# A planned instruction order: searched while the kernel is built, or replayed from a row of stored choices

## The chip, the cores and the metric

The kernel runs on one core of a Trainium2 chip. The metric is the device time in microseconds. TensorE (PE) does the matmuls, VectorE (DVE), ScalarE (ACT) and GpSimd (POOL) the elementwise work, and SyncE (SP) issues most of the transfers. "PEld" in the profile is the weight load of a matmul, which overlaps the matmul before it.

## The reference

The input is 128 graphs of 64 nodes with 256 features (`x`), a 0/1 adjacency of 64 x 64 per graph, and a node mask. Four layers follow one another, and each has the form `x = layernorm(x + layer(x, adj))`:

```python
# layer 0: five rounds of a gated unit
A = (adj != 0)
for l in range(5):
    m   = h @ weight[l]
    agg = einsum('bij,bid->bjd', A, m)
    r, z = sigmoid(...), sigmoid(...)        # of agg @ w_ih.T + h @ w_hh.T + biases
    n    = tanh(i_n + r * h_n)
    h    = (1 - z) * n + z * h
# layer 1: sum over neighbours, W1 (256 -> 1024), RMS norm, silu, W2 (1024 -> 256)
# layer 2: log map, sum over neighbours, exponential map, projection into the ball
# layer 3: attention weights exp(e_i + f_j) masked by adj, normalised, times h = x @ W_w.T + W_b
```

All arithmetic is in float32.

## The kernel before

Two graphs of 64 nodes fill the 128 partitions, with a block-diagonal 128 x 128 adjacency (`edge`). Four such pairs make a group of 8 graphs, and there are 16 groups, numbered 0 to 15. A group goes through all four layers without leaving the chip: load `x`, five gated rounds, then layer 1, 2 and 3, and a store of 512 KB. Nothing passes between groups. Large buffers exist in three sets (`NF = 3`, group number modulo 3), so that a few groups are in flight at any time, at different points of their chain.

The order of the instructions isn't the order of the program text. The functions below only *describe* operations: each call of `flow.op` or `flow.either` records an engine (or two possible engines), an estimated time, the buffers read and written, and a closure that will emit the instruction. A group's operations form one stream. After all streams are described, `Flow.issue` makes a plan: it simulates the five engines with those estimated times and takes, again and again, the operation that could start first among the next few of each stream on each engine. Where several could start at the same time, a ranking decides. There are four rankings: the older stream first; the younger stream first, except for transfers; and two that weigh the length of the chain that still hangs on the operation against the stream's number (`LAGS`, 60 and 150).

The search is over rankings. The planned time is cut into stretches of 37.5 us (`STRETCH`), 10 us near the end (`LAST_STRETCH`). For each stretch every surviving plan is copied and continued with each of the four rankings, and the best 8 (32 near the end) survive by a lower bound of the end (`bound`). The best plan at the end is emitted, with a dependency that keeps each engine in the planned order. Each engine works through its own instructions in that order, and waits for others by semaphores.

Names for the steps that follow:
- `gated` is one round of layer 0. `new_state` (L843) ends it for half of the group: L845 and L847 are two DVE instructions of 128 x 512 that write the new state `hT` (`hN` in the code). `rows_of` (L655) turns the state back into rows on PE, into the bank `ps_hr`; after the fifth round this gives `y0` (L893) and the layer norm that ends layer 0.
- A layer norm has `st`, `mv` and `ve` on DVE, a power on GpSimd (`rstd`, L690), `off` on DVE, and the scaled rows `x_n` on ACT or DVE (L365, L366).
- At the start of layer 1, `aggm` is `x_n` summed over neighbours, and `xb` (L909) is `x_n` plus a bias, 128 x 1024, on GpSimd. The four differences `t` (L934) on DVE feed the products of layer 1. The last two groups (14 and 15) use plain products `ps_hid` in place of these.
- Layer 1 then has the squares `sq` and their sum `sqs`, `ps_ss` and `ps_rms` on PE, scaled and passed through silu into `hid` (L996 on DVE, L998 on ACT), and the product `ps_o`.
- Layer 2 has the factor `fac` and `tan` (L1046), the product `ps_sup`, the squares `junk_a` (L1057), the tanh `th` (L1063) and `y2` (L1079). Layer 3 has `ps_T`, `ps_a`, `hw`, `ps_att`, `rd` and `y3` (L1112).
- `copied` and `scaled` are the operations that either ACT or DVE can do; the plan picks the engine.

Two of the descriptions, with their estimated times:

```python
xb = rows("y", "xb")
pool(2.35, lambda: nc.gpsimd.tensor_tensor(xb.tile(), x1.tile(), over(b2_r.tile(), NB), OP.add), [xb], [x1, b2_r])
# new_state
dve(512, lambda: nc.vector.scalar_tensor_tensor(
    hN[:, :, half(n)], z.tile(), 1.0, hN[:, :, half(n)], OP.add, OP.mult), [(hN, n)], [(hN, n), z])
```

Of the kernel before, what the change touches and what calls it, by code (L numbers as in the profile page):

```python
# [26 lines left out]
class Buf:  # L27


    def __init__(self, make, slot=None, bank=False):  # L30
        self.make, self.slot, self.bank = make, slot, bank
        self.ap, self.uses, self.left, self.after = None, [], 0, ()
# [10 lines left out]
class Op:  # L43
    __slots__ = ("eng", "us", "run", "ways", "stream", "n", "kb", "sets", "need", "then", "bufs", "opens", "id", "way")

    def __init__(self, ways, stream, n, kb, sets):
        self.ways = {eng: (us, run) for eng, us, run in ways}
        self.eng, self.us, self.run = ways[0]
        self.stream, self.n, self.kb, self.sets = stream, n, kb, sets
        self.need, self.then, self.bufs, self.opens, self.id, self.way = 0, [], (), None, 0, 0.0  # L50


class Plan:


    def __init__(self, flow):
        self.flow = flow
        ops = [o for s in flow.streams for o in s]
        self.need = [o.need for o in ops]
        self.at = [0.0] * len(ops)  # L60
        self.uses = {}
        self.clock = dict.fromkeys(flow.AHEAD, 0.75)
        self.queues = [{e: deque(o for o in s if e in o.ways) for e in self.clock} for s in flow.streams]
        self.banks = [0.0] * BANKS
        self.left, self.first, self.bus, self.done = len(ops), 0, 0.0, 0.0
        self.lands = [0.0] * flow.TRANSFERS
        self.past, self.order, self.table = None, [], None

    def copy(self):
        c = Plan.__new__(Plan)  # L70
        c.flow, c.need, c.at, c.uses = self.flow, self.need.copy(), self.at.copy(), self.uses.copy()
        c.clock, c.banks, c.lands = self.clock.copy(), self.banks.copy(), self.lands.copy()
        c.queues = [{e: d.copy() for e, d in q.items()} if self.first <= s < self.first + 2 * self.flow.WINDOW else q
                    for s, q in enumerate(self.queues)]
        c.left, c.first, c.bus, c.done = self.left, self.first, self.bus, self.done
        c.past, c.order, c.table = (self.past, self.order), [], self.table
        return c

    def advance(self, until, rank):


        flow, need, at, clock, banks = self.flow, self.need, self.at, self.clock, self.banks
        while self.left and clock["PE"] < until:
            best = None
            for s in range(self.first, min(self.first + flow.WINDOW, len(self.queues))):
                for e, q in self.queues[s].items():
                    opened = False
                    for _, o in zip(range(flow.AHEAD[e]), q):
                        t = max(clock[e], at[o.id])
                        if o.opens is not None:  # L90
                            if opened or not banks or need[o.id]:
                                opened = True
                                continue
                            t = max(t, banks[0])
                        elif need[o.id]:
                            continue
                        elif o.kb and e != "POOL":
                            t = max(t, self.lands[0])
                        elif o.sets and self.table not in o.sets:
                            t += flow.TABLE  # L100
                        key = (t + flow.SOONER if len(o.ways) > 1 and e == "DVE" else t, *rank(s, o))
                        if best is None or key < best[0]:
                            best = key, o, e, t
            if best is None:
                return False
            _, o, eng, t = best
            if o.sets and self.table not in o.sets:
                self.table = o.sets[0]
            for e in o.ways:
                self.queues[o.stream][e].remove(o)  # L110
            self.order.append((eng, o))
            end = t + o.ways[eng][0]
            clock[eng] = end
            if eng == "PE":
                self.done += o.us
            if o.opens is not None:
                banks.pop(0)
            for b in o.bufs:
                n = self.uses.get(b, b.left) - 1
                self.uses[b] = n  # L120
                if not n:
                    banks.append(end + flow.hop(eng, "PE"))
                    banks.sort()
            if o.kb:
                self.bus = max(self.bus, end + flow.DMA[0]) + o.kb / flow.DMA[1]
                end = self.bus + flow.DMA[2]
                if o.eng != "POOL":
                    self.lands = [*self.lands[1:], end]
            for u in o.then:
                need[u.id] -= 1  # L130
                at[u.id] = max(at[u.id], end + flow.hop(eng, u.eng))
            self.left -= 1
            while self.first < len(self.queues) and not any(self.queues[self.first].values()):
                self.first += 1
        return True

    def bound(self):

        now = self.clock["PE"]
        end = max(now - self.done + self.flow.work, *self.clock.values())  # L140
        for q in self.queues[self.first:]:
            for d in q.values():
                if d:
                    end = max(end, max(self.at[d[0].id], now) + d[0].way)
        return end


class Flow:
# [20 lines left out]
    TRANSFERS = 8  # L169

    TABLE = 1.28
    WINDOW, STRETCH, WIDTH, LAGS = 4, 37.5, 8, (60.0, 150.0,)


    ENDGAME, LAST_STRETCH, LAST_WIDTH = 400.0, 10.0, 32

    BEHIND = mybir.DependencyInfo(mybir.DependencyClass.NoSync, mybir.DependencyReason.DATA)

# [7 lines left out]
    def op(self, eng, us, run, w=(), r=(), kb=0, sets=None):  # L186
        self.either([(eng, us, run)], w, r, kb, sets)

    def either(self, ways, w, r, kb=0, sets=None):

        o = Op(ways, len(self.streams) - 1, len(self.ops), kb, sets)
        before = set()
        for accesses, writes in ((r, False), (w, True)):
# [34 lines left out]
    def ways(self):  # L228

        for i, o in enumerate(o for s in self.streams for o in s):  # L230
            o.id = i
        path = {}
        for ops in self.streams:
            longest = 0.0
            for o in reversed(ops):
                path[o] = o.us + max((path[u] + self.hop(o.eng, u.eng) for u in o.then if u.stream == o.stream), default=0.0)
                o.way = longest = max(longest, path[o])
        self.work = sum(o.us for ops in self.streams for o in ops if o.eng == "PE")

    def issue(self):  # L240
        self.ways()
        ranks = (lambda s, o: (s, o.n), lambda s, o: (s if o.kb else -s, o.n), *(lambda s, o, lag=lag: (lag * s - o.way, s, o.n) for lag in self.LAGS))
        plans, until = [Plan(self)], 0.0
        while any(p.left for p in plans):
            late = until > self.work - self.ENDGAME
            until += self.LAST_STRETCH if late else self.STRETCH
            found = {}
            for p in plans:
                for rank in ranks:
                    c = p.copy()  # L250
                    if c.advance(until, rank):
                        found.setdefault((round(c.bound(), 3), c.left), c)
            plans = [found[k] for k in sorted(found)[:self.LAST_WIDTH if late else self.WIDTH]]
        p, parts = plans[0], []
        past = (p.past, p.order)
        while past is not None:
            parts.append(past[1])
            past = past[0]
        last = {}
        for part in reversed(parts):  # L260
            for eng, o in part:
                made = o.ways[eng][1]()
                for i in made if isinstance(made, list) else [made]:
                    if eng in last:
                        self.tc.add_manual_dep(i.ins, last[eng].ins.name, self.BEHIND, reason="the plan's order")
                    last[eng] = i


@with_exitstack
# [884 lines left out]
```

## Time and profile before

| what | value |
|---|---|
| time, median of three runs | 2415.85 us (2415.77 to 2416.1) |
| span of the profiled execution | 2413.2 us |
| instructions in it | 32774 |
| mean granted TensorE clock | 0.993 of full speed |
| DMA | 36.22 MB, a mean of 15 GB/s |

The page of the profile gives busy times by engine, the span in 40 slices, the chain of work that ended last, and groups of instructions with what they waited for. In a row of the timeline the columns are start in us, duration in us, engine, line, operation, output and inputs with their shape, a count where several were merged, and in brackets how long the engine had stood idle before it and which instruction released it. A row of the waits reads: who waited, for whom, us in total, how often, and the longest.

### The profile page before, as it was taken

To read this page: it belongs to the slowest core of one execution; us is meant where nothing else is said; L and a number is where in the kernel's file an instruction comes from. 1 tells how busy PE (TensorE), PEld (TensorE's weight loads), DVE (VectorE), ACT (ScalarE), POOL (GpSimd) and SP (SyncE) were. 2 spreads that over 40 slices of the span, in tenths; PEclk is the share of its full clock that TensorE was granted. 3 is DMA by queue.
4 is the path that set the end of the run, shared out by engine and by line. 5 is a ranking of instruction groups with operands and counts; after the bars stand their busy time and mean duration, and the time that the engine had idled before them with its cause. 6 is when DMAs were issued, how large, how long until landed. Compare 5 with 4: busy or idle time off the path is not lost.

```text
span 2413.2 us, 32774 instructions
## 1 busy us (share of the span) xinstructions
PE 2364.1 (98%) x12098; PEld 2071.5 (86%) x12098; DVE 1894.3 (78%) x4404; ACT 1211.1 (50%) x2549; POOL 175.1 (7%) x144
## 2 busy tenths in 40 slices
PE   9999999999999999999999999999999999999995
PEld 7888888888888888888888888888888888888764
DVE  5677887878869787887977877878697987888766
ACT  3344554545544555555454455455454544555454
POOL 2000000000000000000000000000010000100001
PEclk9999999999999999999999999999999999999997
DMA  3000000000000000000000000000000000000000
GB/s 121 10 9 3 1 29 1 27 3 1 29 1 29 1 18 12 1 29 1 27 3 1 27 3 4 26 1 29 1 18 12 27 3 1 27 10 18 10 9 18
DMA packets 39727, 36.22 MB, mean 15 GB/s; under 512 B 9956, under 2 KB 38656, under 8 KB 39568
## 3 DMA queue, kind: packets, MB, share of 16 engines
q1 hardware_dynamic: 37840, 32.25, 4.2%
q8 instruction: 96, 1.57, 0.3%
q10 hardware_dynamic: 1328, 1.31, 0.2%
q0 software_dynamic: 400, 0.57, 0.1%
q14 instruction: 63, 0.52, 0.1%
HBM read 25.74 MB, written 8.39 MB: 14 GB/s over the span
## 4 chain that ended last, share of the span: by engine, by line
PE 91%; DVE 6%; ACT 1%; issue 1%; POOL 0%; POOLq 0%; ACTq 0%; DVEq 0%
PE p_v L772 11%; PE p_r L772 11%; PE p_w L772 11%; PE p_in L675 11%; PE ps_o L342 9%; PE ps_agg L342 6%; PE p_hy L783 6%; PE p_u L772 6%; PE p_hx L783 4%; PE ps_hr L655 3%; PE ps_a L342 2%; PE p_wh L938 2%; PE p_vh L938 2%; PE p_1h L938 2%; PE ps_sup L342 1%; PE ps_hid L342 1%
## 5 line engine op out<-in xcount | busy, mean ns | idle before, releaser
L675 PE MATMUL p_in<-agg,w_in 128*128 128x256 f32 x1280 | 321.3, 379 | 0.0
L675 PEld LDWEIGHTS p_in<-agg,w_in 128*128 128x128 f32 x1280 | 242.2, 190 | 33.9 <-issue 1.0
L342 PE MATMUL ps_o<-w2s,hid 128*128 128x256 f32 x1024 | 234.0, 381 | 4.8 <-ACT hid L998 4.8
L342 PEld LDWEIGHTS ps_o<-w2s,hid 128*128 128x128 f32 x1024 | 193.8, 191 | 32.4 <-ACT hid L998 5.9
L690 POOL TENSOR_TENSOR rstd<-ve,pow 128x4 f32<-128x4 f32 (+1 forms) x64 | 83.6, 1306 | 1407.3 <-DVE ve L688 1401.3
L826 ACT ACTIVATE V<-V,half_b 128x256 f32<-128x256 f32 x160 | 73.3, 500 | 195.4 <-DVE V L822 195.4
L772 PE MATMUL p_v<-tA,w_h 128*128 128x256 f32 x640 | 170.0, 379 | 0.5 <-DVE V L822 0.5
L772 PE MATMUL p_r<-hT,w_h 128*128 128x256 f32 x640 | 168.5, 379 | 0.0
L772 PE MATMUL p_v<-tB,w_a 128*128 128x256 f32 x640 | 167.1, 379 | 0.0
L772 PE MATMUL p_r<-agg,w_a 128*128 128x256 f32 x640 | 167.0, 380 | 0.0
L794 DVE SCALAR_TENSOR_TENSOR hnb<-p_hy,half_b,hs 128x256 f32<-128x256 f32 x240 | 108.6, 478 | 46.1 <-PE p_hy L783 45.2
L342 PEld LDWEIGHTS ps_agg<-edge,hr 128*128 128x128 f32 x1024 | 136.8, 191 | 8.2 <-ACT hr L360 0.5
L342 PE MATMUL ps_agg<-edge,hr 128*128 128x128 f32 x1024 | 138.7, 275 | 0.0
L360 ACT COPY agg<-ps_agg 128x512 f32<-128x512 f32 x154 | 89.1, 579 | 98.7 <-PE ps_agg L342 98.2
L360 ACT COPY hr<-ps_hr 128x512 f32<-128x512 f32 x125 | 72.2, 578 | 128.2 <-PE ps_hr L655 127.7
L772 PEld LDWEIGHTS p_v<-tB,w_a 128*128 128x128 f32 x640 | 120.7, 190 | 16.1 <-DVE tB L759 0.2
L772 PEld LDWEIGHTS p_r<-agg,w_a 128*128 128x128 f32 x640 | 119.1, 190 | 15.9 <-issue 0.5
L772 PEld LDWEIGHTS p_v<-tA,w_h 128*128 128x128 f32 x640 | 118.4, 190 | 15.9 <-DVE V L822 1.4
L783 PE MATMUL p_hy<-tA,w_hn 128*128 128x256 f32 x480 | 131.3, 380 | 0.0
L772 PEld LDWEIGHTS p_r<-hT,w_h 128*128 128x128 f32 x640 | 116.6, 190 | 14.0 <-PE ps_hr L655 0.5
L826 ACT ACTIVATE Z<-Z,half_b 128x256 f32<-128x256 f32 x160 | 73.8, 503 | 93.4 <-DVE Z L822 93.2
L826 ACT ACTIVATE U<-U,half_b 128x256 f32<-128x256 f32 x160 | 73.3, 500 | 88.9 <-DVE U L822 88.4
(242 smaller groups left out, 5346.9 us busy)
## 6 DMA issues: line engine op xcount, KB each, us to landing
x<-in_x_dram SPq DMA_DIRECT2D x16, 512.0 KB, 3.6
xr<-in_x_dram SPq DMA_DIRECT2D x16, 512.0 KB, 3.5
out_dram<-x_n SPq DMA_DIRECT2D x16, 512.0 KB, 2.9
edge<-in_adj_dram SPq DMA_DIRECT2D x32, 64.0 KB, 2.3
wm<-in_L_gnn_weight_dram SPq DMA_DIRECT2D x5, 256.0 KB, 5.3
w2s<-in_L_gnn_W_dram SPq DMA_DIRECT2D x1, 1024.0 KB, 9.1
w<-in_L_gnn_W_dram SPq DMA_DIRECT2D x2, 512.0 KB, 3.4
w_in_L_gnn_w_hh_dram<-in_L_gnn_w_hh_dram ACTq DMA_DIRECT2D x1, 512.0 KB, 5.2
```

The costliest lines, as they stand in the source:

```text
L342: return nc.tensor.matmul(o, lhsT, rhs, start=(k == 0), stop=(k == nk - 1))
L360: flow.either([("ACT", 0.22 + 0.00077 * n, lambda: nc.scalar.copy(o(), i())), ("DVE", 0.145 + 0.00105 * n, lambda: nc.vector.tensor_copy(o ...
L655: turn(lambda j=j, c=c: nc.tensor.transpose(ps[:, j * D + c * P:j * D + (c + 1) * P], src[:, c, (2 * n + j) * P:(2 * n + j + 1) * P], iden ...
L675: pe(256, lambda c=c, k=k: nc.tensor.matmul(ps[:, c * HR:(c + 1) * HR], w[:, k, c * P:(c + 1) * P], v(k), start=first and c == k == 0, sto ...
L690: pool(1.1, lambda: nc.gpsimd.tensor_tensor(rstd[:, :m, :], ve[:, :m, :], pow2[:, :m, :], OP.pow), [rstd], [ve])
L772: pe(256, lambda i=i, w=w, c=c: nc.tensor.matmul(ps[:, c * HR:(c + 1) * HR], w[:, m, c * P:(c + 1) * P], v[i][0](), start=first and i == 1 ...
L783: pe(256, lambda: nc.tensor.matmul(ps[:, j * HR:(j + 1) * HR], w_hn[:, m, :], v[1][0](), start=first, stop=True, skip_group_check=True), [ ...
L794: dve(300, lambda: nc.vector.scalar_tensor_tensor(o[0](), ps[:, j * HR:(j + 1) * HR], b(c), x[0](), OP.add, OP.add), [o[1]], [ps, x[1], ha ...
L826: act(256, lambda c=c: nc.scalar.activation(o[:, c, :], src(c), AF.Tanh, bias=half_b[:, i * KD + c:i * KD + c + 1], scale=0.5), [(o, c)], ...
L938: pe(256, lambda c=c: nc.tensor.matmul(ps[:, c * HR:(c + 1) * HR], w1f[:, w, (2 * q + c) * P:(2 * q + c + 1) * P], v[0](), start=first and ...
```

## The change

The search is taken out of the kernel. It was run beforehand, wider and with stretches of 6 us, and its outcome is a row of digits, one per stretch, each naming the ranking to use there. `issue` replays the row: one plan, advanced stretch by stretch with the named ranking, and emitted in the same way as before. What only the search needed (`copy`, `bound`, the counters) goes. The operations, their estimated times, the rankings and the buffers are unchanged. It spares the search when the kernel is built, and gives the search room that it did not have there.

```diff
 class Plan:
-        self.left, self.first, self.bus, self.done = len(ops), 0, 0.0, 0.0
+        self.left, self.first, self.bus = len(ops), 0, 0.0
...
-    def copy(self):
...
-    def bound(self):
...
 class Flow:
-    WINDOW, STRETCH, WIDTH, LAGS = 4, 37.5, 8, (60.0, 150.0,)
-
-
-    ENDGAME, LAST_STRETCH, LAST_WIDTH = 400.0, 10.0, 32
+    WINDOW, STRETCH, LAGS = 4, 6.0, (60.0, 150.0)
+    CHOICES = ("0110020220222022110000000000000120101020000001000000100001011101021010111100022010012111021102110212"
...
+               "112001001101000011110001101111010000101110212211001011110012111101101111002010001101101100101000001")
...
     def issue(self):
...
-        plans, until = [Plan(self)], 0.0
-        while any(p.left for p in plans):
-            late = until > self.work - self.ENDGAME
-            until += self.LAST_STRETCH if late else self.STRETCH
-            found = {}
-            for p in plans:
-                for rank in ranks:
-                    c = p.copy()
-                    if c.advance(until, rank):
-                        found.setdefault((round(c.bound(), 3), c.left), c)
-            plans = [found[k] for k in sorted(found)[:self.LAST_WIDTH if late else self.WIDTH]]
...
+        plan, until = Plan(self), 0.0
+        for c in self.CHOICES:
+            until += self.STRETCH
+            assert plan.advance(until, ranks[int(c)])
+        assert not plan.left
```

More of the change, by code (lines that the diff above doesn't have):

```diff
@@ L64, in __init__ @@
         self.banks = [0.0] * BANKS
-        self.left, self.first, self.bus, self.done = len(ops), 0, 0.0, 0.0
+        self.left, self.first, self.bus = len(ops), 0, 0.0
         self.lands = [0.0] * flow.TRANSFERS
-        self.past, self.order, self.table = None, [], None
-    def copy(self):
[L70 to L77, printed above, removed]
+        self.order, self.table = [], None
     def advance(self, until, rank):
@@ L113, in advance @@
             clock[eng] = end
-            if eng == "PE":
-                self.done += o.us
             if o.opens is not None:
@@ L135, in advance @@
         return True
-    def bound(self):
[L139 to L145, printed above, removed]
 class Flow:
@@ L171 @@
     TABLE = 1.28
-    WINDOW, STRETCH, WIDTH, LAGS = 4, 37.5, 8, (60.0, 150.0,)
-    ENDGAME, LAST_STRETCH, LAST_WIDTH = 400.0, 10.0, 32
+    WINDOW, STRETCH, LAGS = 4, 6.0, (60.0, 150.0)
+    CHOICES = ("0110020220222022110000000000000120101020000001000000100001011101021010111100022010012111021102110212"
+               "1120110110211100000000111110010001121220011022021210001010210110000020000222000000102020202020020121"
+               "1201200002000200002000000021200011121200100100211000010100011012002012000101100110200012101010102210"
+               "112001001101000011110001101111010000101110212211001011110012111101101111002010001101101100101000001")
     BEHIND = mybir.DependencyInfo(mybir.DependencyClass.NoSync, mybir.DependencyReason.DATA)
@@ L237, in ways @@
                 o.way = longest = max(longest, path[o])
-        self.work = sum(o.us for ops in self.streams for o in ops if o.eng == "PE")
     def issue(self):
@@ L242, in issue @@
         ranks = (lambda s, o: (s, o.n), lambda s, o: (s if o.kb else -s, o.n), *(lambda s, o, lag=lag: (lag * s - o.way, s, o.n) for lag in self.LAGS))
-        plans, until = [Plan(self)], 0.0
-        while any(p.left for p in plans):
-            late = until > self.work - self.ENDGAME
-            until += self.LAST_STRETCH if late else self.STRETCH
-            found = {}
-            for p in plans:
-                for rank in ranks:
-                    c = p.copy()
-                    if c.advance(until, rank):
-                        found.setdefault((round(c.bound(), 3), c.left), c)
-            plans = [found[k] for k in sorted(found)[:self.LAST_WIDTH if late else self.WIDTH]]
[L254 to L258, printed above, removed]
-        last = {}
[L260 to L266, printed above, removed]
+        plan, until = Plan(self), 0.0
[3 more added lines that the diff above has]
+        assert not plan.left
+        last = {}
+        for eng, o in plan.order:
+            made = o.ways[eng][1]()
+            for i in made if isinstance(made, list) else [made]:
+                if eng in last:
+                    self.tc.add_manual_dep(i.ins, last[eng].ins.name, self.BEHIND, reason="the plan's order")
+                last[eng] = i
 @with_exitstack
```

## The prediction

> **What bounds the kernel now.** First the row of busy times. TensorE (PE) is at 98%, the next engine, VectorE (DVE), at 78%.
>
> ```profile
> PE 2364.1 (98%) x12098; PEld 2071.5 (86%) x12098; DVE 1894.3 (78%) x4404; ACT 1211.1 (50%) x2549; POOL 175.1 (7%) x144
> ```
>
> The chain of waits agrees (PE 91% of it, DVE 6%). A change of order alone leaves these matmuls as they are, so it can win only what PE stands idle or runs at a lower clock. A table of four stretches (length; busy time of PE, PEld, DVE, ACT, POOL; granted clock; DMA) says where that lies:
>
> ```profile
> 0.00:100.00 100.00, 97.48 (x477) 79.36 (x478) 61.58 (x146) 36.17 (x83) 18.56 (x32) 1.00 0.26 79
> 100.00:2300.00 2200.00, 2188.26 (x11297) 1932.61 (x11296) 1764.17 (x4035) 1119.68 (x2355) 140.16 (x100) 1.00 0.04 12
> 2300.00:2362.50 62.50, 57.40 (x248) 43.78 (x247) 37.98 (x96) 32.38 (x53) 7.02 (x5) 0.97 0.03 9
> 2362.50:2413.20 50.70, 21.00 (x81) 15.78 (x79) 30.62 (x129) 22.87 (x59) 9.35 (x7) 0.69 0.06 21
> ```
>
> Idle PE is 2.5 us at the start, 11.7 us in the 2200 us of the middle, 5.1 us between 2300 and 2362.5 us, and 29.7 us after that, where the last two groups have only short matmuls between long vector chains. Of 49 us in all, most of the last 29.7 us cannot go. Now the waits of PE:
>
> ```profile
> PE ps_T L645 <- ACT x_n L365: 10.2, 1, 10.2
> PE ps_hr L655 <- DVE hT L847: 7.9, 9, 1.5
> PE ps_sup L342 <- ACT tan L1046: 5.9, 1, 5.9
> PE ps_o L342 <- ACT hid L998: 4.8, 2, 4.5
> ```
>
> Three are single waits at the end. The second is the middle: ps_hr waits for the last step of a new state, over and over. The timeline around one of them (start, duration, engine, line) shows why:
>
> ```profile
> 481.79 2.36 POOL L909 TENSOR_TENSOR xb<-x_n,b_r 128x1024 f32<-128x1024 f32 x1 [2.49 <-ACT x_n L365]
> ```
> ```profile
> 482.54 2.16 DVE L845 SCALAR_TENSOR_TENSOR hT<-U,hT 128x512 f32<-128x512 f32 x1 [0.51 <-ACT U L826]
> 484.73 0.69 DVE L847 SCALAR_TENSOR_TENSOR hT<-hT,R 128x512 f32<-128x512 f32 x1
> ```
> ```profile
> 485.57 0.63 PE L655 MATMUL ps_hr<-ident,hT 128*128 128x128 f32 x4 [0.96 <-DVE hT L847]
> ```
>
> L845 takes 2.16 us here and 0.69 us elsewhere. It ends 0.55 us after GpSimd's xb does, 1.47 us late; PE had work for about 0.5 us of that and stood 0.96 us. The plan prices L845 at the same 0.68 us everywhere, so it does not see this. The old plan repeats itself for most groups (these waits come some 145 us apart), and so hits the same spot each time. Last, the end:
>
> ```profile
> 2321.01 2.08 PE L342 MATMUL ps_o<-w2s,hid 128*128 128x256 f32 x4 [4.46 <-ACT hid L998]
> ...
> 2362.50 1.89 PE L342 MATMUL ps_sup<-tan,adjT 128*128 128x256 f32 x8
> 2370.31 3.78 PE L342 MATMUL ps_sup<-tan,adjT 128*128 128x256 f32 x8 [5.92 <-ACT tan L1046]
> 2384.26 2.16 PE L645 MATMUL ps_T<-ident,x_n 128*128 128x128 f32 x8 [10.16 <-ACT x_n L365]
> ```
> ```profile
> 2374.69 0.38 ACT L1057 ACTIVATE junk_a<-ps_sup 128x256 f32<-128x256 f32 x1
> ...
> 2375.19 1.28 ACT L1063 ACT_TABLE_LOAD   x1
> 2376.48 0.30 ACT L1063 ACTIVATE th<-n 128x4 f32<-128x4 f32 x2
> ```
>
> PE waits 4.46 us for group 14's hid, then after the last ps_o for each step of the two groups. ACT does both groups' tanh (th) together, behind group 15's four squares and a table load, though group 14's was ready far earlier.
>
> **What the Trainium skill says.** "SBUF — State Buffer", section "Who interferes with whom": a DVE instruction with two SBUF inputs contends with a GpSimd instruction that reads SBUF, and the later one is blocked until the first is done. L845 has two such inputs, xb too, and 2.16 against 0.69 us agrees. "TensorE: Matmul & The Clock Gate", Part 1: PE's clock is halved after an idle window of some 3.4 us. The trace agrees: the same eight ps_sup take 1.89 us before and 3.78 us after the 5.92 us wait. "ScalarE: Activation LUTs", section "What ACT_TABLE_LOAD costs": about 1283 ns for a load; the trace has 1283 ns.
>
> **The change, part by part.** The search leaves the build and a row of 399 digits picks the rule for each 6 us stretch. By the order of instructions on each engine, built for both kernels, work is neither added nor removed: 6596 matmuls as written in both, 46 table loads in both, and 17 either-engine operations move from DVE (4401 to 4384) to ACT (2490 to 2507). At 0.4 to 0.7 us each that is some 9 us of 1894 us, hidden under PE. The search cost the device nothing. What stays is where things stand.
>
> (a) Start: the first 21 rows on PE are the same; the 2.5 us stay. Further on, most of the first two layers' weight products (ps_wmih) come earlier, in a stretch where PE has no idle time: 0.
>
> (b) Middle. In the old order the pair L845, L847 stands directly ahead of a group's first t<-aggm (L934) in 8 of 14 groups, which is the collision: 8 waits of ps_hr, 7.6 us of the 11.7 us. In the new order it stands there in 3. At 0.95 us each these still cost 2.9 us. The other 11 groups also have one xb each, which will hit some other DVE instruction. In the old trace the six groups outside the pattern lost the rest, 4.1 us or 0.69 us a group, part of it other small misses. I take 0.5 us for each of the eleven, a little under that, since a search with shorter stretches should leave PE more ready work: 5.5 us. Middle 8.4 us, a gain of 3.3 us. Bounds: at 0.69 us the gain is 1.2 us; with nothing lost at the eleven it is 8.8 us.
>
> (c) The wait for hid. In the old order group 14's ps_o had only a few transposes of group 15 beside it. Idle there is 4.46 + 0.26 + 0.30 us and the slower clock after it makes 4 matmuls and 16 ps_agg take 2.08 + 2.56 us instead of some 1.03 + 1.95 us: 6.7 us in all. In the new order both groups' ps_hid come first, 13 of group 15's stand between group 14's ps_ss and ps_rms, and ps_ss of group 15 follows. Then PE waits for group 15's last copy, square and add (0.58 + 0.72 + 0.69 us, less 0.44 us of ps_rms): 1.6 us; and, as the silu table load (1.28 us) and first silu (0.72 us) stand behind that square on ACT, some 0.4 us more after ps_ss. With x_n of group 15 and its aggm copies between ps_hid (1 to 1.5 us) I take 3.4 us. Gain 3.3 us, from 1 to 6.
>
> (d) The last chain. The new order on ACT puts the table load and group 14's th ahead of group 15's squares, in the time PE needs for ps_sup. It can start when tan of group 15 is done, 2371.1 us on the old scale: load to 2372.3, th to 2372.5, six small DVE steps of 0.2 us to 2373.7, against 2377.9 us before: 4 us earlier, and with it group 14's ps_T, 10.16 us of wait. Behind it, group 15's chain gives part back: its x_n is now four ACT instructions behind group 14's hw (before: split between ACT and DVE), about 1 us, and x_n of group 14 stands late, so that both output transfers meet: some 0.5 us more. On DVE the block of 0.83 us before off of group 14 goes. I take 3.0 us, from 1 to 4.5.
>
> Sum: 3.3 + 3.3 + 3.0 = 9.6 us, 2415.85 to **2406.2 us**.
>
> **The rivals.** *Tail only:* every xb finds a victim again and the middle stays at 11.7 us. For it: 16 xb, 2.4 us each, and DVE at 78%. Against: six groups of the old trace lost less. 2415.85 − 6.3 = 2409.5 us. *Nearly everything goes:* the middle falls to 2 us, the hid wait to 1 us, the chain gains 4.5 us: 9.7 + 5.7 + 4.5 = 19.9 us, 2396 us. Against: the plan still prices no collision. *Slower:* the new order has no repeating pattern; groups stand closer together at times (reloads xr of groups 2 and 3 almost meet on the queue), so that it could lose in more places. If all 14 groups lost the longest wait seen, 1.48 us, and half of them a second of 0.96 us, the middle would be 27.4 us, 15.7 more; less 6.3 us at the end this gives 2425 us. Against: nothing in the old trace loses twice as a rule.
>
> **How the numbers follow.** Likeliest case 60%, tail only 15%, nearly everything 10%, slower 15%. The range 2396.5 to 2414.5 us leaves out half of the third case (5%) and the slower one (15%). Bound (0.2%): 2411.0 and 2420.7 us. Below it lie the first and third and two thirds of the second case, 80%; within it 9%, from the second and the milder part of the fourth; above it 11%.
>
> **What would show it.** After: PE busy time as before; ps_hr waiting for hT in about 3 places, not 9; idle in the middle near 8 us; a wait of ps_o for hid under 3 us and the clock at 1.00 there; th of group 14 before group 15's squares, and the wait of ps_T near 6 us. Wrong if the middle loses more than 12 us, by many small waits of PE for DVE or ACT, or if tail waits merely move from ps_T to the last group.

## The result and the profile after

The changed kernel takes **2407.89 us** (median of four runs, 2406.22 to 2409.2) where the kernel before, on the same chip, takes 2415.97 us (2415.77 to 2417.17). The ratio is 0.9966, with a 95% interval from 0.9952 to 0.998: 8.1 us, or 0.34%, faster. The forecast was 2406.2 us, with a range from 2396.5 to 2414.5 us. The profiled executions of the two differ by 9.1 us (2413.2 and 2404.1 us; that of the changed kernel is the fastest of its four runs), and the readings below account for those 9.1 us.

The lines of the changed kernel carry numbers 34 lower than those of the kernel before: L811 and L813 are the two steps of hT that were L845 and L847, L875 is xb, L900 is t, L611 the transposes ps_T, L1029 is th. First the row of busy times, which shows the same matmuls on an engine that is as busy as before:

```profile
PE 2362.7 (98%) x12098; PEld 2071.9 (86%) x12098; DVE 1886.2 (78%) x4387; ACT 1222.5 (51%) x2566; POOL 173.6 (7%) x144
```

Then the table of four stretches of the changed kernel (start and end; length; busy time and count of PE, PEld, DVE, ACT, POOL; granted clock; DMA share and GB/s):

```profile
0.00:100.00 100.00, 97.23 (x481) 79.66 (x482) 61.66 (x143) 38.30 (x86) 18.93 (x32) 1.00 0.26 78
100.00:2300.00 2200.00, 2188.88 (x11316) 1937.86 (x11315) 1757.83 (x4027) 1125.48 (x2365) 138.76 (x100) 1.00 0.04 12
2300.00:2360.00 60.00, 56.75 (x231) 39.86 (x230) 36.91 (x92) 36.06 (x58) 7.42 (x5) 1.00 0.00 1
2360.00:2404.10 44.10, 19.83 (x76) 14.55 (x74) 29.81 (x128) 22.64 (x58) 8.49 (x7) 0.73 0.07 24
```

Length less PE's busy time is its idle time. It was 2.5, 11.7, 5.1 and 29.7 us in the four stretches, and is 2.8, 11.1, 3.3 and 24.3 us now: 49.0 us have become 41.4. So of 7.6 us of idle time that went, 5.4 lie in the last stretch, 1.9 in the one before it, and only 0.6 in the long middle. PE's busy time fell by another 1.4 us, because fewer matmuls run at the lower clock (0.97 has become 1.00 in the third stretch, 0.69 has become 0.73 in the last). The waits of PE of the changed kernel name the places (who waited, for whom; us in total, times, longest):

```profile
PE ps_sup L308 <- DVE tan L1011: 5.9, 1, 5.9
PE ps_T L611 <- ACT x_n L331: 5.8, 1, 5.8
PE p_wh L904 <- DVE t L900: 3.8, 4, 1.3
PE p_hx L749 <- DVE tA L725: 3.6, 2, 2.3
...
PE ps_ss L308 <- DVE sqs L892: 2.1, 1, 2.1
PE ps_hid L308 <- ACT aggm L326: 1.1, 1, 1.1
PE p_uh L904 <- DVE t L900: 1.1, 1, 1.1
PE ps_agg L308 <- ACT x_n L331: 1.0, 1, 1.0
PE p_hy L749 <- DVE hnb L760: 0.9, 1, 0.9
PE ps_hr L621 <- DVE hT L813: 0.3, 1, 0.3
```

Compare with the list of the kernel before. The wait of ps_T has gone from 10.2 to 5.8 us, the wait of ps_o for hid is gone, and the nine waits of ps_hr for hT (7.9 us) have become one of 0.3 us. But p_wh and p_uh, which waited 2.2 us for t before, now wait 4.9 us, and p_hx waiting for tA, p_hy for hnb and ps_agg for x_n are new, 5.5 us. The middle has changed its waits, not lost them.

Last, PE's timeline at the end of the changed kernel:

```profile
2312.07 2.84 PE L308 MATMUL ps_hid<-aggm,w 128*128 128x512 f32 x6 [1.15 <-ACT aggm L326]
...
2329.50 1.05 PE L308 MATMUL ps_ss<-ones,sqs 128*128 128x1 f32 x8 [2.10 <-DVE sqs L892]
2330.43 10.81 PE L308 MATMUL ps_o<-w2s,hid 128*128 128x256 f32 x48
...
2358.78 1.89 PE L308 MATMUL ps_sup<-tan,adjT 128*128 128x256 f32 x8
2366.58 3.70 PE L308 MATMUL ps_sup<-tan,adjT 128*128 128x256 f32 x8 [5.91 <-DVE tan L1011]
2376.09 2.17 PE L611 MATMUL ps_T<-ident,x_n 128*128 128x128 f32 x8 [5.82 <-ACT x_n L331]
```

The 48 ps_o in this row run through without a stop, at 0.225 us each, where the granted clock is 1.00 in the table. The wait for tan (5.91 us) is what it was, since group 15's chain up to tan takes as long as before (7.80 us from the first ps_sup to the second, and 7.81 before); the wait for group 14's x_n behind it is 4.3 us shorter. From the start of the second ps_sup to the end of the span it is 37.5 us (2404.1 less 2366.58), where it was 42.9 us.

### Why the middle stays: two kinds of waits

Between 100 and 2290 us the waits of PE come to 11.1 us before and 10.4 us after. The trace has two kinds of them in the new order. Here is the first, three engines around 1217 us in the changed kernel:

```profile
1217.30 2.36 POOL L875 TENSOR_TENSOR xb<-x_n,b_r 128x1024 f32<-128x1024 f32 x1 [4.60 <-ACT x_n L331]
```
```profile
1218.05 2.15 DVE L811 SCALAR_TENSOR_TENSOR hT<-U,hT 128x512 f32<-128x512 f32 x1 [1.67 <-ACT U L792]
```
```profile
1221.41 0.67 PE L904 MATMUL p_wh<-t,w1f 128*128 128x256 f32 x2 [1.26 <-DVE t L900]
```

The DVE step takes 2.15 us beside xb, as its twin did before. It now stands further ahead of the product that ends up waiting: hT itself is no longer what PE waits for, but t, which DVE makes after it. There are seven waits beside xb in the middle, five for t and one each for tA and hnb, 7.1 us in all; before there were 10.3 us.

The second kind isn't a collision at all. Around 548 us in the changed kernel:

```profile
548.38 0.42 DVE L725 TENSOR_TENSOR tA<-hT 128x256 f32<-128x256 f32 x1 [2.73 <-DMA out_dram<-x_n]
```
```profile
549.41 0.67 PE L749 MATMUL p_hx<-tA,w_hn 128*128 128x256 f32 x2 [2.33 <-DVE tA L725]
```

tA takes the buffer from which a finished group is still being written out. DVE stands for 2.73 us until that transfer has landed, and PE behind it for 2.33 us. The same happens near 1214 us, where tA waits 1.62 us for an output transfer, `off` stands behind it on DVE, and x_n and ps_agg come 0.98 us late. The plan gives the transfer 0.1 us and so reckons with a buffer that is free almost at once. These two waits, 3.3 us, weren't there before: the old order lists no wait of DVE for an output transfer, the new one five, 5.6 us in all, of which PE feels two.

### The profile page after: what moved, and what is told of

Its sections match the earlier page's. It is cut to its first block, busy times and chain, and to the rows that moved or that the text cites. A ratio compares the mean times of both kernels' runs of the same rounds, so it can differ in the third digit from the quotient of the medians.

```text
span 2404.1 us, 32737 instructions
## 1 busy us (share of the span) xinstructions
PE 2362.7 (98%) x12098; PEld 2071.9 (86%) x12098; DVE 1886.2 (78%) x4387; ACT 1222.5 (51%) x2566; POOL 173.6 (7%) x144
## 4 chain that ended last, share of the span: by engine, by line
PE 90%; DVE 6%; ACT 2%; issue 1%; POOL 1%; DMA 0%; POOLq 0%; ACTq 0%; DVEq 0%
PE p_v L738 11%; PE p_w L738 11%; PE p_in L641 11%; PE p_r L738 10%; PE ps_o L308 9%; PE ps_agg L308 6%; PE p_hy L749 5%; PE p_u L738 5%; PE p_hx L749 4%; PE ps_hr L621 3%; PE ps_a L308 2%; PE p_wh L904 2%; PE p_vh L904 2%; PE p_1h L904 2%; PE ps_T L611 1%
## 5 line engine op out<-in xcount | busy, mean ns | idle before, releaser
L641 PE MATMUL p_in<-agg,w_in 128*128 128x256 f32 x1280 | 327.3, 380 | 0.0
L308 PE MATMUL ps_o<-w2s,hid 128*128 128x256 f32 x1024 | 229.0, 379 | 0.0
L760 DVE SCALAR_TENSOR_TENSOR hnb<-p_hy,half_b,hs 128x256 f32<-128x256 f32 x240 | 108.3, 478 | 37.5 <-PE p_hy L749 36.5
L805 ACT ACTIVATE R<-R,cols 128x256 f32<-128x256 f32 x160 | 73.0, 501 | 78.4 <-DVE R L803 77.9
```

Of the source, the lines that this page charges most:

```text
L308: return nc.tensor.matmul(o, lhsT, rhs, start=(k == 0), stop=(k == nk - 1))
L641: pe(256, lambda c=c, k=k: nc.tensor.matmul(ps[:, c * HR:(c + 1) * HR], w[:, k, c * P:(c + 1) * P], v(k), start=first and c == k == 0, sto ...
L760: dve(300, lambda: nc.vector.scalar_tensor_tensor(o[0](), ps[:, j * HR:(j + 1) * HR], b(c), x[0](), OP.add, OP.add), [o[1]], [ps, x[1], ha ...
L805: act(256, lambda c=c: nc.scalar.activation(t[:, c, :], t[:, c, :], AF.Tanh, bias=bih(2 * KD + c)), [(t, c)], [(t, c), cols], TANH)
```

## The experiments

The account to be tested: in the middle the new order loses about 3 us less beside xb, gives that back to output transfers, and gains in the last 90 us, at hid and in the last chain; two moves of the last chain can be undone by hand. The rivals: that the middle's waits have another cause than xb; that the last chain's gain comes from ACT alone; that the shorter stretches or the wider search by themselves bring the gain. Edits of the old order are made on a replay of it from a row of its own choices; *before_th*, built so, has the old order's waits in the middle (7.6 us for hT, 1.9 us for t) and its time. The kernel before took 2415.6 to 2416.0 us on every chip used, so times from different chips are set side by side below.

### xb taken apart, and taken away

Three edits of line L909 (L875), the sum of residual and bias:

```diff
-pool(2.35, lambda: nc.gpsimd.tensor_tensor(xb.tile(), x1.tile(), over(b2_r.tile(), NB), OP.add), [xb], [x1, b2_r])
 # before_split, after_split: four pieces of 128x256
+pool(2.35, lambda: [nc.gpsimd.tensor_tensor(xb[:, b, :], x1[:, b, :], b2_r.tile(), OP.add) for b in range(NB)], [xb], [x1, b2_r])
 # after_split8: eight pieces of 128x128
+pool(2.35, lambda: [nc.gpsimd.tensor_tensor(xb[:, b, k * P:(k + 1) * P], x1[:, b, k * P:(k + 1) * P], b2_r[:, k * P:(k + 1) * P], OP.add)
+                    for b in range(NB) for k in range(2)], [xb], [x1, b2_r])
 # before_mem, after_mem: written without reading
+pool(2.35, lambda: nc.gpsimd.memset(xb.tile(), 0.0), [xb], [x1, b2_r])
```

The two kernels with the memset, which fills the tile with zeros, leave out the residual and the bias of layer 1; every other instruction and its place stay.

**before_split**, the old order with xb in four pieces:

> The old order, with GpSimd's xb (128 x 1024, 2.36 us) issued as four additions of 128 x 256; nothing else moves. Theory A (the waits of PE in the middle come from DVE instructions blocked while xb runs): a block is at most one quarter, some 0.65 us, where it was 1.47 us; eight waits of 0.67 to 1.48 us leave almost nothing, and the idle time of PE in the middle falls from 11.1 us to 2 or 3 us; the time falls by 7 to 9 us to about 2408 us. Rival B (the plan's margins are short in general and xb only happens to run then): within 1.5 us of before.

Measured: 2408.68 us, ratio 0.997 (0.9959 to 0.9981), 7.2 us faster. The waits in the middle fall from 11.1 to 4.3 us, not quite to the 2 or 3 us expected. The timeline of this kernel around the place that the prediction showed, GpSimd and then DVE:

```profile
480.84 3.69 POOL L909 TENSOR_TENSOR xb<-x_n,b_r 128x256 f32<-128x256 f32 x4 [2.49 <-ACT x_n L365]
```
```profile
481.60 1.21 DVE L845 SCALAR_TENSOR_TENSOR hT<-U,hT 128x512 f32<-128x512 f32 x1 [0.52 <-ACT U L826]
482.84 1.10 DVE L847 SCALAR_TENSOR_TENSOR hT<-hT,R 128x512 f32<-128x512 f32 x1
483.86 0.95 DVE L934 TENSOR_TENSOR t<-aggm 128x256 f32<-128x256 f32 x1
```

DVE and GpSimd take turns. The first step of hT is held for one piece (1.21 us, where 0.69 is its free duration and 2.16 was its time before), and the next two DVE instructions for another part each. In sum DVE is held as long as before (0.52 + 0.41 + 0.53 us against 1.47), but only the first two stand ahead of hT, which is done 2.34 us after L845 starts instead of 2.88. GpSimd pays for it (3.69 us for the four pieces instead of 2.36), and no listed wait of any engine is for xb. In the waits of PE of this kernel the longest wait for hT is 0.4 us:

```profile
PE ps_hr L655 <- DVE hT L847: 2.7, 7, 0.4
```

**after_split**, the same in the new order:

> The new order, with the same split of xb. Theory A: of 10.4 us of waits in the middle, 2.33 us at 549 us is a wait for an output transfer and 0.98 us at 1216 us one for x_n; the other 7.1 us are behind xb and fall to about 1.5 us: some 5.5 us less than the new order as it is, about 2402 us. Rival B: within 1.5 us of the new order.

Measured: 2400.79 us, ratio 0.9938 (0.9926 to 0.9951): 7.1 us under the new order's 2407.89. The middle's waits are 6.8 us, of which 3.3 are the two behind output transfers, unmoved by this edit. Beside xb 3.5 us are left, where 1.5 were expected, and still the time fell by more than expected; the last section comes back to this.

**before_mem**, the old order with nothing for GpSimd to read:

> The old order, with xb replaced by a fill of the same tile with zeros on GpSimd: it leaves out the residual and the bias of layer 1, and no longer reads SBUF, so that by theory A it blocks no DVE instruction with two inputs at all. Theory A: the idle time of PE in the middle falls from 11.1 to 1 or 2 us, about 2406 us, a little below the split. Rival C (GpSimd blocks DVE by any access, writing too): the eight waits stay in part, as far as the fill is as long as xb was. Rival B: no change.

Measured: 2402.11 us, ratio 0.9942 (0.9929 to 0.9954), 13.8 us faster. The middle's waits are 0.97 us. So nearly all that the old order lost there was xb. The memset is also shorter than xb, 0.95 us in the same place, so the fall by itself doesn't say whether it is the reading or the length that counts. But a DVE step with two inputs can be seen beside a memset, in group 0:

```profile
193.31 0.95 POOL L909 MEMSET xb<- 128x1024 f32 x1 [3.32 <-ACT x_n L365]
```
```profile
193.68 0.69 DVE L845 SCALAR_TENSOR_TENSOR hT<-U,hT 128x512 f32<-128x512 f32 x1 [0.50 <-ACT U L826]
```

It starts while GpSimd writes and takes its free 0.69 us: writing the tile doesn't hold DVE, and what the memset lacks is xb's reading. The page "SBUF — State Buffer" of the Trainium skill, section "Who interferes with whom", says that a DVE instruction with two SBUF inputs contends with a GpSimd instruction that reads SBUF and not with one that only writes; this run agrees: 0.69 us beside the memset, 2.16 us beside xb.

**after_mem**, the new order with the same memset:

> The new order, with xb replaced by a fill with zeros (the residual and the bias of layer 1 left out). Theory A: 7 us of the 10.4 us in the middle go, the 2.33 us and 0.98 us stay: about 2401 us. If the two orders with the fill differ by the 8 us by which they differ with xb, the gain of the new order is all at the end; if they differ by less, part of it was luck with xb.

Measured: 2395.68 us, ratio 0.9917 (0.9904 to 0.9931), 12.2 us under the new order, where 7 us were expected. These two waits are all that PE has left in the middle (100 to 2290 us) of this kernel:

```profile
PE p_hx L749 <- DVE tA L725: 2.3, 1, 2.3
PE ps_agg L308 <- ACT x_n L331: 1.0, 1, 1.0
```

They are the two behind output transfers. So the split of the middle into kinds holds: in the old order 10.3 us of listed waits belong to xb and 0.8 to the rest; in the new one 7.1 and 3.3.

One more wait goes with xb, and it lies behind the middle: the 1.15 us of ps_hid for aggm, which neither after_split nor after_mem has. In the changed kernel DVE's sqs (L892) starts at 2308.45 us beside group 15's xb (2307.88 to 2310.24) and takes 2.34 us instead of 0.69; ACT's next square waits for it, and behind that square on ACT stands the copy into aggm. So over the whole kernel the listed waits beside xb are 10.3 us in the old order and 8.2 in the new, 2.1 less. The spans of the profiles agree: taking xb away shortens the old order by 12.8 us and the new one by 10.8.

With xb out of both orders the new one is still 6.4 us ahead (2402.11 less 2395.68; 7.1 us by the profiles). By the traces it should be 4.6 at hid (6.7 less the 2.1 that are left) and 5.4 in the last chain, less 2.3 in the middle and 0.3 at the start: 7.4 us.

**after_split8**, eight pieces in the new order:

> The new order with xb in eight additions of 128 x 128 where the version in four gave 2400.8 us. If what counts is how long one block holds DVE up, blocks half as long leave PE some 1 to 2 us less to wait for: about 2399.5 us, with the floor at the 2395.7 us of the version whose GpSimd doesn't read. If every further GpSimd instruction costs DVE a turn of its own (DVE and GpSimd take turns while xb runs), the sum of the blocks stays the same or grows with the count, and it is 2401 to 2403 us.

Measured: **2398.12 us** (2395.81 to 2400.47), ratio 0.9926 (0.9912 to 0.9939). This is 9.8 us under the new order and 17.9 us under the kernel before (2416.03 us on that chip), and the fastest median of the kernels that leave nothing out; its interval overlaps that of four pieces (0.9926 to 0.9951). The waits of PE in its middle:

```profile
PE p_hx L749 <- DVE tA L725: 2.3, 1, 2.3
PE ps_agg L308 <- ACT x_n L331: 1.0, 1, 1.0
PE p_wh L905 <- DVE t L901: 0.6, 2, 0.4
PE p_uh L905 <- DVE t L901: 0.3, 1, 0.3
```

Of the 7.1 us beside xb 0.9 remain, where four pieces left 3.5: of the two cases expected, it is the one in which the length of one block counts. Smaller pieces cost GpSimd more (two of 128x128 take 1.18 us on average, where one of 128x256 took 0.89), but GpSimd has room: 9% busy.

### The last chain

The new order differs from the old at the end in many places. Two of them could be moved by hand, in the finished order: on ACT, the table load and th of group 14 stand ahead of group 15's four squares; on DVE, two small steps of group 15 (n and rn), the first of which waits for GpSimd, no longer stand ahead of group 14's steps from th to its y. In the edit, `of(g, k)` is the k-th operation after the power of group g, and `move` puts operations ahead of another in the order:

```diff
+        move([of(14, 2)], of(15, -6))                                                # before_th
+        move([of(14, 2)], of(15, -6)); move([of(15, k) for k in (1, 2, 3)], of(15, 4))  # before_th_dve
+        move([of(15, k) for k in (*range(-8, 0), 0, 1, 3)], of(14, 2))               # after_th_back, in the new order
```

**before_th**, the old order with the move on ACT alone:

> The old order with one move at the end: on ACT, the table load and group 14's th stand ahead of group 15's four squares (junk_a), as in the new order; DVE keeps its order, where n and rn of group 15 stand ahead of group 14's six small steps. Theory A (ACT's order is the gain of the last chain): 3 to 4 us less, about 2412.5 us. Rival D (DVE is in order too, so group 14's steps still wait behind n of group 15, which needs all of its squares and GpSimd's power): within 1 us of before, since th is then early and nobody can use it, or even some tenths later, as the load can delay the squares.

Measured: 2415.59 us beside 2415.72, ratio 1.0 (0.9992 to 1.0008): nothing. ACT does what was wanted, as its timeline in this kernel shows: th of group 14 starts at 2373.69 us, where it starts at 2376.48 in the trace of the kernel before:

```profile
2372.40 1.28 ACT L1065 ACT_TABLE_LOAD   x1
2373.69 0.20 ACT L1065 ACTIVATE th<-n 128x4 f32<-128x4 f32 x1
```

But DVE takes no notice. Its timeline in the same kernel:

```profile
2377.61 0.16 DVE L1064 SCALAR_TENSOR_TENSOR n<-n 128x4 f32<-128x4 f32 x1 [6.11 <-POOL n L1063]
...
2377.91 0.13 DVE L1071 TENSOR_TENSOR th<-th,rn 128x4 f32<-128x4 f32 x1
```

The first line is group 15's, waiting 6.11 us for GpSimd's root; the second is group 14's first use of th, which has been ready since 2373.9 us and stands behind it. It was ready and did not pass the one that waited on its own engine. The prediction had put the gain of the last chain on ACT's order; alone that order is worth nothing. The trace of the kernel before shows why, on DVE:

```profile
2376.29 0.16 DVE L1062 SCALAR_TENSOR_TENSOR n<-n 128x4 f32<-128x4 f32 x1 [6.11 <-POOL n L1061]
2376.49 0.18 DVE L1075 RECIPROCAL rn<-n 128x4 f32<-128x4 f32 x1
2376.72 0.16 DVE L1069 TENSOR_TENSOR th<-th,rn 128x4 f32<-128x4 f32 x1
```

There group 14's first use of th starts at 2376.72 us. ACT makes that th from 2376.48 us on, in about 0.2 us, and group 15's rn ends on DVE at 2376.67 us. Two gates stand before group 14, and they open at the same moment. By this trace a move on DVE alone would have gained next to nothing too; that is an estimate, since no run makes that move alone.

**before_th_dve**, the old order with both moves:

> The old order with both moves: th of group 14 ahead on ACT, and on DVE n and rn of group 15 behind group 14's layer norm sums, as in the new order. Both theories: group 14's y begins some 4 us earlier, the wait of ps_T falls from 10.2 to about 6 us, and the time by 3 to 5 us, about 2412 us. If this gives the new order's whole gain behind the last ps_o (5.3 us by the traces), the last chain is explained; what is short of it lies in the later differences (rd, x_n, off).

Measured: 2412.57 us, ratio 0.9986 (0.9979 to 0.9992), 3.2 us faster. The wait of ps_T in this kernel:

```profile
PE ps_T L648 <- ACT x_n L368: 6.9, 1, 6.9
```

It was 10.2 us. **after_th_back**, the new order with both moves undone:

> The new order with both moves undone: th of group 14 behind group 15's squares on ACT, and n and rn of group 15 ahead of group 14's steps on DVE. The wait of ps_T goes from 5.8 back to about 10 us, and the time up by 3 to 5 us, to about 2412 us. If it stays near 2408 us, the gain of the end lies elsewhere.

Measured: 2411.7 us, ratio 0.9982 (0.9975 to 0.9989), 3.8 us over the new order, and the wait of ps_T is back:

```profile
PE ps_T L625 <- ACT x_n L345: 9.9, 1, 9.9
```

So the two moves together are some 3 to 4 us of the 5.4 us that the last chain gained. The other 1.6 to 2.2 us lie in the many later differences of the two orders and weren't taken apart.

### The search

Which of the two things brings the gain, the shorter stretches or the wider search? The width of the search behind the new row isn't known, so four others were run ahead of the build and replayed in the kernel before's code:

```diff
-    WINDOW, STRETCH, WIDTH, LAGS = 4, 37.5, 8, (60.0, 150.0,)   # kernel before; last 400 us: 10.0 and 32
+    STRETCH, WIDTH = 6.0, 8       # short8, 6.0 to the end
+    WIDTH = 64                    # wide64, old stretches
+    STRETCH, WIDTH = 6.0, 64      # short64, 6.0 to the end
 # short64_lock: short64, with a plan that knows xb's grip on DVE
+    if e == "DVE" and self.held[0] <= t < self.held[1]:
+        t = self.held[1]
...
+    if eng == "POOL" and o.us == 2.35:
+        self.held = (t, end)
```

**short8:**

> The old search (8 survivors, all four rankings, the same bound) with stretches of 6 us throughout, its outcome replayed: shorter stretches without a wider search. If the short stretches are what helps, it comes near the new order, about 2408 us; if the width does, it stays near 2416 us or worse, since 8 survivors of stretches of 6 us see a shorter way ahead. In both cases I expect the middle to lose 8 to 12 us, since no search sees what xb does to DVE.

Measured: 2427.09 us, ratio 1.0049 (1.0035 to 1.0063), 11.4 us slower. Its profile is that of its slowest run (2431.21 us). The middle's waits are 11.1 us, as before; the loss is at the end, where PE stands idle for 9.5 us around hid and 11.3 us ahead of ps_T.

**wide64:**

> The old search with its old stretches (37.5 us, 10 us near the end) but 64 survivors where it had 8 and 32: width without shorter stretches. The short stretches with 8 survivors gave 2427 us, 11 us over before. If width is what the new order owes its gain to, this comes to 2408 to 2412 us, with the gain at the end; if it takes both, it stays within 3 us of before. The middle loses 8 to 12 us of listed waits as in every order so far.

Measured: 2413.14 us, ratio 0.999 (0.9982 to 0.9999), 2.5 us faster, within the 3 us that were expected if width alone is not enough. Its waits of PE show a middle like the old one (11 waits for hT), and at the end the new order's wait of ps_T:

```profile
PE ps_hr L643 <- DVE hT L835: 10.4, 11, 1.5
PE ps_T L633 <- ACT x_n L353: 5.8, 1, 5.8
```

**short64:**

> The search with stretches of 6 us and 64 survivors throughout, both of the new order's changes to the search (its own width is not known). If the two together are what is needed, about 2408 us like the new order, and at most 2412 us. If it stays near the 2427 us of 8 survivors, the new order's search differed in more than that. The middle again loses 8 to 12 us.

Measured: 2417.1 us, ratio 1.0006 (0.9998 to 1.0014), not to be told from no change, where some 2408 us were expected. The first 179 digits of its row are those of the new row, so up to there the two searches chose alike. The middle's waits are 11.3 us and, up to 950 us, stand in the new order's places; but ps_T waits 11.3 us.

**short64_lock:**

> The same search, 6 us and 64 survivors, with one thing added to the plan: a DVE operation that would start while xb runs on GpSimd starts only when xb has ended (for every DVE operation, though by the traces it holds for those with two inputs in SBUF). xb itself stays whole. If the collisions can be planned around, the waits of PE in the middle fall from 10 or 11 us to 2 to 5 us, and this is 5 to 9 us faster than the same search without it. If no free places of 2.4 us exist on DVE, the plan moves the loss about and the two stay within 2 us.

Measured: 2412.15 us, ratio 0.9985 (0.9978 to 0.9991), 3.5 us under the kernel before and 5.0 under short64. No wait of the middle stands beside xb any longer, so the plan can be taught to step around it. Yet 8.6 us of waits are left there, where 2 to 5 were expected, and the four big ones follow waits like these two, on DVE in this kernel:

```profile
1353.14 0.42 DVE L752 TENSOR_TENSOR tA<-hT 128x256 f32<-128x256 f32 x1 [3.11 <-DMA out_dram<-x_n]
...
1641.40 0.43 DVE L752 TENSOR_TENSOR tA<-hT 128x256 f32<-128x256 f32 x1 [3.35 <-DMA out_dram<-x_n]
```

DVE waits 12.2 us for output transfers here, 5.6 us in short64 and in the new order, and not at all in the old one. With the one cost priced, this search leaned on the next one that isn't: the output transfer at 0.1 us. A version that prices the transfer too wasn't tried.

The four searches end anywhere from 2412 to 2427 us. Among the orders whose plan doesn't know of xb, the middle's waits are all 10 to 12 us, and what tells them apart is the end that they happened to find: behind 2290 us the waits of PE come to 15.0 us in the new order, 17.8 in wide64, 20.8 in short64, 21.3 in the kernel before and 25.2 in short8. Neither short stretches nor width brings the 8 us by itself, nor do the two together at a width of 64. What in the search behind the new row found its end stays open.

## Why the prediction was right, and where it wasn't

**The sum came out: 9.6 us were forecast, 9.1 us are in the profiles and 8.1 us in the medians. The terms did not all.**

- *(a) the start, 0:* idle time there rose from 2.5 to 2.8 us. Right within 0.3 us.
- *(b) the middle, 3.3 us (1.2 to 8.8):* **mis-sized**; it is 0.7 us, under the lower bound. The part of it that was worked out came out in sum: waits beside xb in the middle went from 10.3 to 7.1 us, 3.2 us less, and they were put at 3.3. What the step left out is that the order decides when tA takes over a buffer under an output transfer; this cost 3.3 us in two places. The medians of the pairs give 13.8 and 12.2 us for xb in the two orders, 1.6 us less with intervals of some 3 us either way; the wait of 1.15 us in (c), which is xb's too, goes the same way. The means were a guess that averaged well: in the middle seven of the xb cost PE 0.4 to 1.3 us each and the others nothing that is listed, not 0.95 in three groups and 0.5 in eleven.
- *(c) the wait for hid, 3.3 us (1 to 6):* right in size, and in cause for the larger part. Idle time and slower clock came to 6.7 us before; after, PE waits 1.15 us for aggm and 2.10 us for sqs, 3.25 us, and ps_o for hid not at all, with the clock at 1.00. The gain is 3.4 us. The 2.10 us are the copy, square and add that were put at 1.6 us. The 1.15 us were foreseen as x_n and copies of aggm, but are one more DVE step behind xb. No run undoes this part by itself; it rests on the two traces.
- *(d) the last chain, 3.0 us (1 to 4.5):* **mis-sized, and with half a cause**. It is 5.4 us, over the upper bound. The wait of ps_T fell by 4.3 us, as the 4 us of the working say; but the 1.5 us that group 15's chain was to give back didn't come: from PE's last matmul to the end it is 12.4 us now and was 13.4. And the working put the 4 us on ACT's order and does not name DVE's wait of 6.11 us; its 0.83 us on DVE are a later wait, ahead of off. *before_th* gives nothing and *before_th_dve* 3.2 us: ACT's order and DVE's block were two gates that opened together, and the working saw one.

The two errors, 2.6 us too much in (b) and 2.4 us too little in (d), cancel. That the total was close is therefore partly luck; the profile showed the places, and for (c) the size.

Of the signs that the prediction named, these came: th of group 14 ahead of the squares, ps_T near 6 us (5.8), no wait of ps_o, clock 1.00, and PE busy as before. The middle near 8 us of idle time did not (11.1), nor did ps_hr waiting for hT in three places: the one wait of 0.3 us that is left stands at 88 us, away from any xb, and none of the seven waits beside xb is of that kind. *Tail only*, at 2409.5 us, is the rival that the profile after comes closest to: the middle hardly moved. It is off in its reason: fewer xb make PE wait, seven in the middle where it was twelve. *Slower* had the right fear, an order with no pattern that brings groups closer together, and short8, at 2427 us, shows that such an order can be slower; but it loses at the end, while its middle lists the same 11.1 us.

## What to carry to other kernels

A plan can avoid only what it prices; here it left out the grip of GpSimd's xb on DVE and a buffer held by an output transfer. Before searching longer, look in the trace for operations that take longer than their price and for waits that the plan has at zero, and either price them or take the cause away; here cutting one GpSimd instruction into eight brought 9.8 us on top of the 8.1 us of the search. When a chain is to be shortened by moving one instruction, follow it on to the next engine: it is early for nothing if its user stands behind another wait there. Two waits that end at the same moment have to go together.

## What the runs showed of the hardware

- *In pieces, GpSimd and DVE take turns.* One xb of 2.36 us held one DVE step for 1.47 us; in four pieces it held three steps for about 0.5 us each, and took 3.69 us itself.
- *A GpSimd memset of the same tile held nothing.* A DVE step with two inputs took 0.69 us beside it, and the middle's waits were 0.97 us with 16 memsets of 0.95 us.
- *A wait of PE cost more here than the idle time listed for it.* From the kernel before to before_mem the first y of one group after another comes 2.38, 3.53 and 4.68 us earlier, 1.15 us per group, where the wait that was taken away is listed with 0.96 us. Over the whole middle the listed waits fell by 10.2 us and the first ps_sup of group 15 came 12.8 us earlier. Where the other 0.2 us per wait go wasn't settled; part of it may be in the modelled ends of the matmuls.
